# Attention diagonal by four products instead of a DRAM round trip, and other moves in the first 45 microseconds of a four-layer graph kernel

## Chip, cores and metric

One Trainium2 chip, one of its cores. The metric is the device time of one execution in microseconds (us), median of several runs of the same program; lower is better. The engines of the core work side by side and wait for each other by semaphores: PE is TensorE (matrix products; PEld loads its weights), DVE is VectorE, ACT is ScalarE, POOL is GpSimd, and SP is the queue that asks for transfers (DMA). Products land in PSUM, eight banks of 128x512 float32.

## The reference, cut to what matters

`x` has 32 batches of 512 nodes with 128 features, `adj` is 512x512. Four layers follow each other, each of the form x = x + layer(relu(layernorm(x))). Only the first layer, and its preparation, is touched by the change:

```python
# --- layer 0, as computed on h = relu(layernorm(x)) ---
h0 = jnp.einsum('bnf,fg->bng', h, W[0])
h1 = jnp.einsum('bnf,fg->bng', h, W[1])
m = adj > 0
idx = jnp.cumsum(m.reshape(-1).astype(jnp.int32)) - 1      # running number of the non-zeros
A = softmax(jnp.where(m, e[0][idx], NEG), axis=1)          # the attention matrix, 512 x 512
M = jnp.eye(512)
out = einsum('ij,bjg->big', A * M, h0) + einsum('ij,bjg->big', A * (1 - M), h1) + bias
# layer 1: Chebyshev hops with adj; layer 2: messages with adj*adj; layer 3: masked attention
```

So layer 0 needs the attention matrix without its diagonal (it multiplies h1), and its diagonal by itself: row i of h0 is scaled by A[i, i].

## The kernel before: the parts that the change touches

Batches are handled in pairs, q = 0 to 15, and two pairs make a round r. The kernel is written in the order in which each engine works its instructions off in this part, so the order of lines below is the order on each engine. Blocks of 128 nodes are numbered t.

The inputs are asked for on one queue, and the statistics of the first two pairs are made by DVE and POOL together:

```python
for t in range(NT):
    nc.sync.dma_start(adj_s[:, t, :], adj_r[:, t, :])
# then, on the same queue: x of the first batches, q, k, e, the weights, the other x
...
def early_stats(q, whole):
    for b in range(2):
        for k in range(2 * b, 2 * b + 2):
            nc.vector.bn_stats(st[:, k], xt[q][:, b, ...])
        if whole and b == 0: yield; continue
        nc.vector.tensor_scalar(sd[:, half], st[:, half, :, 2], 1.0 / D, EPS, OP.mult, OP.add)
        nc.vector.tensor_scalar(sh[:, half], st[:, half, :, 1], -1.0, None, OP.mult)
        nc.gpsimd.tensor_tensor(rs[:, half], sd[:, half], minus_half[:, half], OP.pow)
        nc.gpsimd.tensor_mul(sh[:, half], sh[:, half], rs[:, half])
        yield
```

`normal[q]` are the eight ACT instructions that make h of pair q from x, shift and scale. `pe_steps` (`turned[q]`) turns h of a pair: eight PE transposes into two banks at the first step, then a copy of each bank into hT. `project_steps` (`project[q]`) multiplies hT with W[1] into two banks, and copies both into g. Then comes the numbering of the non-zeros, with the turning of pair 0 behind it:

```python
pw = [bank(f"p_upto_{kk}") for kk in range(NK)]            # running sums, NK = 2
for kk in range(NK):
    for j in range(NT): nc.tensor.matmul(pw[kk][:, j * P :], pgs[:, j, blk(kk)], upto[:, j, j * P :], ...)
turned = [pe_steps(h[q], f"hT0_{q}", hT[q], copies[q]) for q in range(3)]
next(turned[0])                                            # eight transposes of pair 0
next(early[1])
for kk in range(NK):                                       # column of each of the first 256 non-zeros
    nc.vector.tensor_scalar(s, pw[kk], rest[:, kk : kk + 1], None, OP.is_le, OP.add, accum_out=col_of[...])
for kk in range(NK):                                       # one-hots of row and column
    nc.vector.tensor_scalar(at_row[:, kk, :], cols, row_of[:, kk : kk + 1], None, OP.is_equal)
    nc.vector.tensor_scalar(at_col[:, kk, :], cols, col_of[:, kk : kk + 1], -1.0, OP.is_equal, OP.mult)
for kk in range(NK):
    for i in range(3): nc.vector.tensor_scalar(at_part[:, i, kk, :], ...)
go(turned[0])                                              # both ACT copies of pair 0
next(project[0])                                           # products of pair 0 with W[1]
go(normal[1])
```

For each block of rows t the scores are made on PE from the one-hots (`score_rows`), the softmax by DVE and ACT (`softmax_rows`, `inverse`, `scaled_rows`), and the diagonal is cut out and summed:

```python
def scaled_rows(t):
    nc.scalar.mul(split(att[:, t, :]), crossed(us[t]), total[:, t : t + 1])

def without_diagonal(t):
    own = split(att[:, t, :])[:, :, t, :]                  # the block that holds the diagonal
    d = diag[:, t, :]
    nc.vector.tensor_tensor_reduce(d, own, ident, 1.0, 0.0, OP.mult, OP.add, diag_of[:, t : t + 1])
    nc.gpsimd.tensor_sub(own, own, d)
...
without_diagonal(3)
...
# diag_of has one number per node, nodes along the partitions; adiag has all 512 along the free
# dimension, the same on every partition. The way from one to the other leads through DRAM:
nc.sync.dma_start(diag_d.rearrange("(t p) -> p t", p=P), diag_of)
nc.sync.dma_start(adiag[0], AP(diag_d, ap=[[0, P], [1, N]]))
```

Round 0 multiplies the attention matrix with g in seven block products (a Strassen scheme, `ORDER0`: k = 1, 2, 6, 5, 7, 4, 3). Other work is placed behind each of them:

```python
if i == 0:   # behind k = 1
    transpose_rows(pt, att, 2); transpose_rows(pt, att, 3); copies of attT, block sums on DVE
elif i == 1: # behind k = 2
    go(normal[2], NT + 1); diagonal_of(0, 0); go(ln3, NT + 1); go(normal[2]); ...
elif i == 2: # behind k = 6
    diagonal_of(0, 1); add(1, 0, 0)
elif i == 3: # behind k = 5
    turn pair 2 (PE, ACT copies); add(0, 1, 1); bias(0); normalise(3); ...
elif i == 4: # behind k = 7
    upper(held["a"]); turn pair 3; add(1, 1, 2); go(projection(2)); normalise(4); bias(1); ...
elif i == 5: # behind k = 4
    go(projection(3)); go(right_of(1)); diagonal_of(1, 0); normalise(5)
```

`diagonal_of(r, b)` makes hd = hT * adiag on POOL for both pairs of the round (128x512 each). `upper` multiplies hd with W[0] on PE and adds the result to x on DVE; `add` and `bias` are POOL additions of 128x512 into x; `right_of(1)` are the four POOL differences of g that round 1 needs. After round 0 the kernel goes on through seven more rounds of layer 0 and through layers 1 to 3.

Of the kernel before, what the change touches and what calls it, by code (L numbers as in the profile page):

```python
# [16 lines left out]
P = 128  # L17
# [7 lines left out]
def kernel(  # L25
# [51 lines left out]
    def bank(name):  # L77
        return psum.tile([P, 512], F32, tag="bank", name=name)
# [4 lines left out]
    def blk(t):  # L83
        return slice(t * P, (t + 1) * P)
# [17 lines left out]
    adj_s = square_tile("adj_s")  # L102
    adj_r = adj.rearrange("(t p) j -> p t j", p=P)
    for t in range(NT):
        nc.sync.dma_start(adj_s[:, t, :], adj_r[:, t, :])

    xq, xt = [], []

# [70 lines left out]
    nc.scalar.activation(prep.tile([P, 1], F32, name="powers"), eps, AF.Exp)  # L179
    minus_half = const.tile([P, NT, 2], F32, name="minus_half")  # L180
    nc.vector.memset(minus_half, -0.5)

    known = prep.tile([P, NT, 2], F16, name="known")
    nc.vector.tensor_copy(known[:, :, 1], rows)
# [11 lines left out]
    def early_stats(q, whole):  # L196

        st = stats.tile([P, NT, 2, 3], F32, tag="bn", name=f"bn_{q}", bufs=4)
        sd = stats.tile([P, NT, 2], F32, tag="sd", name=f"sd_{q}", bufs=4)
        rs = stats.tile([P, NT, 2], F32, tag="rs", name=f"rs_{q}")  # L200
        sh = stats.tile([P, NT, 2], F32, tag="sh", name=f"sh_{q}")
        shift[q] = sh.rearrange("p k e -> p (k e)")
        scale[q] = rs.rearrange("p k e -> p (k e)")
        for b in range(2):
            for k in range(2 * b, 2 * b + 2):
                t = 2 * k % NT
                nc.vector.bn_stats(st[:, k].rearrange("p e s -> p (e s)"),
                                   xt[q][:, b, t : t + 2, :].rearrange("p t f -> p f t"))
            if whole and b == 0:
                yield  # L210
                continue
            half = slice(0 if whole else 2 * b, 2 * b + 2)
            nc.vector.tensor_scalar(sd[:, half], st[:, half, :, 2], 1.0 / D, EPS, OP.mult, OP.add)
            nc.vector.tensor_scalar(sh[:, half], st[:, half, :, 1], -1.0, None, OP.mult)
            nc.gpsimd.tensor_tensor(rs[:, half], sd[:, half], minus_half[:, half], OP.pow)
            nc.gpsimd.tensor_mul(sh[:, half], sh[:, half], rs[:, half])
            yield
# [41 lines left out]
    def pe_steps(h, name, hT, copy=nc.scalar.copy):  # L259
        ps = [bank(f"p_{name}_{b}") for b in range(2)]  # L260
        for b in range(2):
            for t in range(NT):
                nc.tensor.transpose(ps[b][:, blk(t)], h[:, b, t, :], ident)
        yield
        for b, p in enumerate(ps):
            (copy[b] if isinstance(copy, tuple) else copy)(
                hT[:, :, b, :].rearrange("p b (a c) -> p b a c", c=QR), crossed(p))
            yield
# [178 lines left out]
    def project_steps(q, hT, copy=nc.scalar.copy):  # L447
        r, w = divmod(q, 2)
        if w == 0:
            if r % 3 == 2:  # L450
                g[r] = square_tile(f"g_{r}").rearrange("p t (b w f) -> p t b w f", b=2, w=2)
            else:
                t = quad_tile(f"g_{r}").rearrange("p w e -> p (w e)")[:, : 4 * N]
                g[r] = t.rearrange("p (t b w f) -> p t b w f", t=NT, b=2, w=2)
        pg = [projected(f"p_g_{q}_{b}", (at(hT, b), w0[:, 1, :])) for b in range(2)]
        yield
        for b in range(2):
            copy(g[r][:, :, b, w, :], pg[b])
            yield
# [122 lines left out]

    rest = prep.tile([P, NK], F32, name="rest")
    nc.vector.tensor_sub(rest, rows[:, :NK], pb[:, :, 0])
    pw = [bank(f"p_upto_{kk}") for kk in range(NK)]
    for kk in range(NK):
        for j in range(NT):
# [1 line left out]
                             start=(j == 0), stop=(j == NT - 1), skip_group_check=True)  # L589
    copies = [nc.scalar.copy, (nc.scalar.copy, nc.vector.tensor_copy), nc.scalar.copy]  # L590
    turned = [pe_steps(h[q], f"hT0_{q}", hT[q], copies[q]) for q in range(3)]
    project = [project_steps(q, hT[q], c) for q, c in ((0, nc.scalar.copy), (1, nc.vector.tensor_copy))]
    next(turned[0])
    col_of = prep.tile([P, NK], F32, name="col_of")
    at_row = prep.tile([P, NK, N], BF16, name="at_row")
    at_col = prep.tile([P, NK, N], BF16, name="at_col")
    at_part = prep.tile([P, 3, NK, N], BF16, name="at_part")
    us = [prep.tile([P, N], F32, tag="u", name=f"u_{t}", bufs=NT) for t in range(NT)]
    next(early[1])
    for kk in range(NK):  # L600
        s = prep.tile([P, N], F16, tag="scr", name=f"scr_c{kk}", bufs=2)
        nc.vector.tensor_scalar(s, pw[kk], rest[:, kk : kk + 1], None, OP.is_le, OP.add,
                                accum_out=col_of[:, kk : kk + 1])
    for kk in range(NK):
        nc.vector.tensor_scalar(at_row[:, kk, :], cols, row_of[:, kk : kk + 1], None, OP.is_equal)
        nc.vector.tensor_scalar(at_col[:, kk, :], cols, col_of[:, kk : kk + 1], -1.0, OP.is_equal, OP.mult)
    for kk in range(NK):
        for i in range(3):
            nc.vector.tensor_scalar(at_part[:, i, kk, :], cols, col_of[:, kk : kk + 1],
                                    parts[i][:, kk : kk + 1], OP.is_equal, OP.mult)  # L610
    go(turned[0])
    next(project[0])
    go(normal[1])


    diag = prep.tile([P, NT, P], F32, name="diag")
    diag_of = prep.tile([P, NT], F32, name="diag_of")
    least = prep.tile([P, NT], F32, name="least")
    total = prep.tile([P, NT], F32, name="total")

# [21 lines left out]

    def scaled_rows(t):
        nc.scalar.mul(split(att[:, t, :]), crossed(us[t]), total[:, t : t + 1])

    def without_diagonal(t):

        own = split(att[:, t, :])[:, :, t, :]
        d = diag[:, t, :].rearrange("p (b c) -> p b c", c=QR)
        nc.vector.tensor_tensor_reduce(d, own, ident.rearrange("p (b c) -> p b c", c=QR), 1.0, 0.0,  # L650
                                       OP.mult, OP.add, diag_of[:, t : t + 1])
        nc.gpsimd.tensor_sub(own, own, d)

    attT = square_tile("attT")
# [12 lines left out]
    softmax_rows(2)  # L667
    inverse(1)
    scaled_rows(1)
    without_diagonal(0)  # L670
    score_rows(3)
    next(turned[1])
    next(turned[1])
    softmax_rows(3)
    without_diagonal(1)
    inverse(2)
    scaled_rows(2)
    go(early_stats_2, 2)
    inverse(3)
    scaled_rows(3)  # L680
    next(project[1])
    without_diagonal(2)
    pt = [bank(f"p_attT_{j}") for j in range(NT)]
    transpose_rows(pt, att, 0)
    transpose_rows(pt, att, 1)
    next(project[1])
    without_diagonal(3)
    next(project[1])

    adiag = [work.tile([P, N], F32, tag="rt", name="adiag", bufs=6)]  # L690
    diag_d = bounce.tile([N], F32, tag="diag", name="diag_d", bufs=1)
    tc.keep_in_program_order(nc.sync.dma_start(diag_d.rearrange("(t p) -> p t", p=P), diag_of))
    tc.keep_in_program_order(nc.sync.dma_start(
        adiag[0], bass.AP(tensor=diag_d.tensor, offset=diag_d.offset, ap=[[0, P], [1, N]])))
    left_of_att = att_sums()
    next(left_of_att)
    att_copies((0, 0, nc.scalar.copy), (1, 0, nc.vector.tensor_copy),
# [37 lines left out]

    ahead = {q: stats_steps(q) for q in range(4, NQ)}
    ln3 = stats_steps(3)
    own, turning, hd = {}, {}, {}
    sums_ahead = late_sums()

    def normalise(q):
# [34 lines left out]
    def round0(r):  # L776

        now = rights.pop(r)  # L780
        A, C = 2 * r, 2 * r + 1

        def x_of(I, b):
# [41 lines left out]
        for i, _ in enumerate(products(f"l0_{r}", by_token, sums["att"], now, evict,  # L825
                                          ORDER if r else ORDER0)):
            if r == 0:
                if i == 0:
                    transpose_rows(pt, att, 2)
                    transpose_rows(pt, att, 3)  # L830
                    att_copies((0, 1, nc.scalar.copy), (1, 1, nc.vector.tensor_copy))
                    next(left_of_att)
                    next(left_of_att)
                    go(early_stats_2)
                    att_copies((2, 1, nc.scalar.copy), (3, 1, nc.scalar.copy))
                elif i == 1:
                    go(normal[2], NT + 1)
                    diagonal_of(0, 0)
                    go(ln3, NT + 1)
                    go(normal[2])  # L840
                    next(left_of_att)
                    next(left_of_att)
                    next(squares)
                    go(ln3)
                elif i == 2:
                    diagonal_of(0, 1)
                    add(1, 0, 0)
                elif i == 3:
                    next(turned[2])
                    go(turned[2])  # L850
                    add(0, 1, 1)
                    bias(0)
                    normalise(3)
                    go(ahead[4], NT)
                    go(squares)
                elif i == 4:
                    upper(held["a"])
                    turned.append(pe_steps(h[3], "hT0_3", hT[3]))
                    next(turned[3])
                    go(ahead[4])  # L860
                    add(1, 1, 2)
                    go(turned[3])
                    go(projection(2))
                    normalise(4)
                    go(ahead[5], NT)
                    bias(1)
                    go(turn(4))
                    go(ahead[5])
                elif i == 5:
                    go(projection(3))  # L870
                    go(right_of(1))
                    diagonal_of(1, 0)
                    normalise(5)
                elif i == 6:
                    go(stats_c, NT)
                continue
# [326 lines left out]
```

## Time and profile before

| | before |
|---|---|
| time, median of 3 runs (lowest to highest) | 971.69 us (971.6 to 972.12) |
| span of the profiled execution | 969.8 us |
| PE busy | 956.3 us, 99% |
| PEld busy | 782.4 us, 81% |
| DVE busy | 586.8 us, 61% |
| ACT busy | 469.3 us, 48% |
| POOL busy | 419.4 us, 43% |
| mean granted clock of PE | 0.996 |

A row of the stage table gives, for a stretch of the span, how long each engine was busy in it (in brackets the number of instructions), the clock that PE was granted as a share of full speed, the busy share of the transfer engines, and what they moved. A row of the waits gives an instruction, what it waited for, the total in us, how often, and the longest. A row of an engine's timeline gives start, duration, engine, line, operation, what it writes and reads, how many instructions are merged in it, and in square brackets how long the engine stood idle before it and for whom. "L773" is line 773 of the kernel before. Busy time of an engine that runs beside PE costs nothing by itself; it matters where PE waits for it.

### The profile page before, as it was taken

Reading aid. Unit: us, or ns where it says so; the run is one execution under the profiler, and the core shown is the slowest. Engines: PE = TensorE matmul, PEld = TensorE weight load, DVE = VectorE, ACT = ScalarE, POOL = GpSimd, SP = SyncE. Lnnn points to the kernel's source line nnn. Section 1 sums busy time; section 2 is a strip of 40 time slices with the busy share of each in tenths; the row PEclk is TensorE's granted clock in tenths of the full one; section 3 lists DMA queues with packets and bytes.
Section 4 is the critical chain, followed back from the end, with each engine's and each line's share of the span. In section 5 each row is a group of like instructions: output and inputs, shape, how many; then the busy total and the mean of one; then the engine's idle time right before and its main releaser. Section 6 shows DMA issues by size and latency. Waiting matters only on the chain.

```text
span 969.8 us, 15152 instructions
## 1 busy us (share of the span) xinstructions
PE 956.3 (99%) x5461; PEld 782.4 (81%) x5461; DVE 586.8 (61%) x1339; ACT 469.3 (48%) x1054; POOL 419.4 (43%) x459
## 2 busy tenths in 40 slices
PE   8899999999999999999999999999999999999998
PEld 4699999989999998899887777777676777777776
DVE  8778886746555546646757666656654454454444
ACT  5674442442341242376636744455664445544553
POOL 4486998834328523511424444334042233223322
PEclk9899999999999999999999999999999999999999
DMA  9345643252232321433342432232231121221111
GB/s 250 71 119 164 183 122 110 58 139 66 80 120 62 88 49 39 131 92 102 75 119 81 142 88 70 83 88 75 56 98 55 53 73 51 60 71 44 55 33 44
DMA packets 84586, 86.32 MB, mean 89 GB/s; under 512 B 7328, under 2 KB 75168, under 8 KB 84512
## 3 DMA queue, kind: packets, MB, share of 16 engines
q1 hardware_dynamic: 84512, 85.36, 31.4%
q8 instruction: 43, 0.70, 0.3%
q14 instruction: 31, 0.25, 0.1%
HBM read 44.44 MB, written 40.90 MB: 88 GB/s over the span
## 4 chain that ended last, share of the span: by engine, by line
PE 93%; DVE 3%; DMA 2%; ACT 1%; issue 0%; SPq 0%; POOL 0%; DVEq 0%; ACTq 0%
PE p_av L1123 12%; PE p_score L1108 11%; PE p_l_c L384 8%; PE p_w L433 6%; PE p_l_d L384 5%; PE p_msgT_c L377 4%; PE p_x1T_c L377 4%; PE p_l_a L384 4%; PE p_l L433 3%; PE p_feat L433 3%; PE p_hv L433 3%; PE p_qkh L1095 3%; PE p_x1T_a L377 3%; PE p_msgT_d L377 3%; PE p_x1T_d L377 3%; PE p_msgT_a L377 3%
## 5 line engine op out<-in xcount | busy, mean ns | idle before, releaser
L245 ACT ACTIVATE h<-x,sh,rs 128x128 f32<-128x128 f32 x512 | 209.1, 485 | 54.8 <-DVE sh L234 23.9
L1113 POOL TENSOR_TENSOR ex<-ex,adjTx 128x512 f32<-128x512 f32 x62 | 80.3, 1296 | 208.2 <-ACT ex L1111 208.2
L1109 ACT ACTIVATE ex<-p_score 128x512 f32<-128x512 f32 x128 | 71.8, 587 | 122.9 <-issue 113.1
L1123 PEld LDWEIGHTS p_av<-qkh_hv,ex 128*128 128x128 f32 x1024 | 118.4, 191 | 8.4 <-issue 7.4
L1123 PE MATMUL p_av<-qkh_hv,ex 128*128 128x129 f32 x1024 | 119.9, 274 | 0.0
L1108 PE MATMUL p_score<-qkh_hv,hT 128*128 128x512 f32 x256 | 115.2, 593 | 0.0
L281 DVE STREAM_TRANSPOSE hb_hT<-h 128x512 f32<-128x512 f32 x120 | 82.0, 698 | 23.6 <-ACT h L245 23.2
L1113 DVE TENSOR_TENSOR ex<-ex,adjTx 128x512 f32<-128x512 f32 x66 | 46.1, 702 | 82.0 <-ACT ex L1111 81.9
L225 DVE BATCH_NORM_STATS2 bn<-x 128x6 f32<-128x256 f32 x248 | 89.7, 416 | 0.6
L1108 PEld LDWEIGHTS p_score<-qkh_hv,hT 128*128 128x128 f32 x256 | 46.2, 190 | 46.5 <-issue 44.5
L1111 ACT ACTIVATE ex<-ex 128x512 f32<-128x512 f32 x128 | 76.6, 630 | 1.8
L354 POOL TENSOR_TENSOR rt_feat<-feat,feat 128x256 f32<-128x256 f32 x16 | 11.6, 726 | 136.3 <-ACT feat L1062 136.3
L956 ACT COPY w<-p_w 128x512 f32<-128x512 f32 x32 | 18.2, 574 | 105.6 <-PE p_w L433 105.6
L354 POOL TENSOR_TENSOR rt_w<-w,rt_w 128x512 f32<-128x512 f32 x16 | 20.4, 1276 | 110.2 <-DVE rt_w L354 91.8
L433 PE MATMUL p_w<-th,x1T 128*128 128x128 f32 x256 | 49.5, 275 | 0.0
L433 PE MATMUL p_w<-th,hs 128*128 128x128 f32 x256 | 49.5, 275 | 0.0
L433 PEld LDWEIGHTS p_hv<-vw,hT 128*128 128x128 f32 x256 | 33.6, 192 | 15.3 <-issue 8.1
L1073 POOL TENSOR_TENSOR x<-x,phi2b 128x256 f32<-128x256 f32 x64 | 44.5, 727 | 0.0
L717 POOL TENSOR_TENSOR hd<-hT,adiag 128x512 f32<-128x512 f32 x32 | 39.7, 1276 | 8.2 <-DMA adiag<-diag_d 8.2
L433 PEld LDWEIGHTS p_w<-th,hs 128*128 128x128 f32 x256 | 39.9, 192 | 0.7
L1128 DVE SCALAR_TENSOR_TENSOR x<-p_av,rsum,x 128x128 f32<-128x128 f32 x128 | 39.1, 346 | 1.9
L1062 ACT ACTIVATE feat<-feat 128x512 f32<-128x512 f32 x32 | 20.1, 629 | 41.4 <-DVE feat L1061 41.4
(231 smaller groups left out, 2041.4 us busy)
## 6 DMA issues: line engine op xcount, KB each, us to landing
d_hT<-hb_hT SPq DMA_DIRECT2D x240, 128.0 KB
hT<-d_hT SPq DMA_DIRECT2D x60, 512.0 KB
x<-in_x_dram SPq DMA_DIRECT2D x32, 256.0 KB
out_dram<-x SPq DMA_DIRECT2D x31, 256.0 KB
adj_s<-in_adj_dram SPq DMA_DIRECT2D x4, 256.0 KB
adjT_d<-adj_squares SPq DMA_DIRECT2D x4, 256.0 KB
sq<-in_adj_dram SPq DMA_DIRECT2D x4, 256.0 KB
adjTx<-adjT_d SPq DMA_DIRECT2D x4, 256.0 KB
```

Of the source, the lines that this page charges most:

```text
L225: nc.vector.bn_stats(st[:, k].rearrange("p e s -> p (e s)"), xt[q][:, b, t : t + 2, :].rearrange("p t f -> p f t"))
L245: nc.scalar.activation(h[:, b, t, :], xt[q][:, b, t, :], AF.Relu, bias=shift[q][:, i : i + 1], scale=scale[q][:, i : i + 1])
L281: nc.vector.transpose(hb[:, :, b].rearrange("p j t r -> p t j r"), h[:, b].rearrange("p t (j c) -> p t j c", c=QR))
L377: nc.tensor.matmul(p[:, :H], b[:, k, :], a[:, k, :], start=(first and k == 0), stop=(k == 1), skip_group_check=True)
L384: nc.tensor.matmul(p[:, i * 2 * D : (i + 1) * 2 * D], a[:, k, blk(i)], b[:, k], start=(first and i == 0 and k == 0), stop=(k == 1), skip_g ...
L433: nc.tensor.matmul(p[:, blk(t)], hT(t), w, start=(i == 0), stop=(i == len(terms) - 1))
L1073: tc.keep_in_program_order(nc.gpsimd.tensor_add(xi, xi, spread(phi2b, 2)))
L1108: nc.tensor.matmul(ps, hT[:, t, b, :], qkh, start=True, stop=True)
L1109: nc.scalar.activation(ex[:, t, :], ps, AF.Tanh, scale=1.0 / (8.0 * math.sqrt(D)))
L1111: nc.scalar.activation(ex[:, t, :], ex[:, t, :], AF.Exp, scale=8.0)
L1113: eng.tensor_mul(split(ex[:, t, :]), split(ex[:, t, :]), crossed(adjTx[0][:, t, :]))
L1123: nc.tensor.matmul(po[:, i, : D + 1], ex[:, t, blk(i0 + i)], hv[:, t, :], start=(t == 0), stop=(t == NT - 1))
```

## The change

Four things are altered. **First**, blocks 1 and 3 of `adj` are asked for on ACT's queue and blocks 0 and 2 on SP's, so that the loads of `x` behind them are asked for sooner. **Second**, the two small steps between the statistics and the power (`sd`, `sh`) and one of the four one-hots of row and column (`at_row[1]`) go from DVE to POOL. **Third**, pair 0 is turned batch by batch: batch 0 before the running sums (its copy behind ACT's copy of `pgs`), batch 1 behind them. **Fourth**, the diagonal block is cut out by a plain POOL multiplication, straight after the row is scaled, and the row of all diagonals on every partition is made by PE: a matrix of ones times the diagonal block leaves the sum of each column, which is the diagonal itself, on every partition. Four such products go into a bank behind k = 2 of round 0, and one ACT copy brings the bank to `adiag`. The sums `diag_of` and the two transfers through DRAM are gone.

```diff
--- before.py
+++ after.py
@@ -102,7 +102,7 @@
     adj_s = square_tile("adj_s")
     adj_r = adj.rearrange("(t p) j -> p t j", p=P)
     for t in range(NT):
-        nc.sync.dma_start(adj_s[:, t, :], adj_r[:, t, :])
+        (nc.scalar if t % 2 else nc.sync).dma_start(adj_s[:, t, :], adj_r[:, t, :])
 
     xq, xt = [], []
 
@@ -179,6 +179,8 @@
     nc.scalar.activation(prep.tile([P, 1], F32, name="powers"), eps, AF.Exp)
     minus_half = const.tile([P, NT, 2], F32, name="minus_half")
     nc.vector.memset(minus_half, -0.5)
+    ones = const.tile([P, P], F32, name="ones")
+    nc.vector.memset(ones, 1.0)
 
     known = prep.tile([P, NT, 2], F16, name="known")
     nc.vector.tensor_copy(known[:, :, 1], rows)
@@ -210,8 +212,8 @@
                 yield
                 continue
             half = slice(0 if whole else 2 * b, 2 * b + 2)
-            nc.vector.tensor_scalar(sd[:, half], st[:, half, :, 2], 1.0 / D, EPS, OP.mult, OP.add)
-            nc.vector.tensor_scalar(sh[:, half], st[:, half, :, 1], -1.0, None, OP.mult)
+            nc.gpsimd.tensor_scalar(sd[:, half], st[:, half, :, 2], 1.0 / D, EPS, OP.mult, OP.add)
+            nc.gpsimd.tensor_scalar(sh[:, half], st[:, half, :, 1], -1.0, None, OP.mult)
             nc.gpsimd.tensor_tensor(rs[:, half], sd[:, half], minus_half[:, half], OP.pow)
             nc.gpsimd.tensor_mul(sh[:, half], sh[:, half], rs[:, half])
             yield
@@ -582,6 +584,13 @@
 
     rest = prep.tile([P, NK], F32, name="rest")
     nc.vector.tensor_sub(rest, rows[:, :NK], pb[:, :, 0])
+    def turn_first(b):
+        p = bank(f"p_hT0_0_{b}")
+        for t in range(NT):
+            nc.tensor.transpose(p[:, blk(t)], h[0][:, b, t, :], ident)
+        nc.scalar.copy(hT[0][:, :, b, :].rearrange("p b (a c) -> p b a c", c=QR), crossed(p))
+
+    turn_first(0)
     pw = [bank(f"p_upto_{kk}") for kk in range(NK)]
     for kk in range(NK):
         for j in range(NT):
@@ -589,32 +598,32 @@
                              start=(j == 0), stop=(j == NT - 1), skip_group_check=True)
     copies = [nc.scalar.copy, (nc.scalar.copy, nc.vector.tensor_copy), nc.scalar.copy]
     turned = [pe_steps(h[q], f"hT0_{q}", hT[q], copies[q]) for q in range(3)]
+    turn_first(1)
     project = [project_steps(q, hT[q], c) for q, c in ((0, nc.scalar.copy), (1, nc.vector.tensor_copy))]
-    next(turned[0])
     col_of = prep.tile([P, NK], F32, name="col_of")
     at_row = prep.tile([P, NK, N], BF16, name="at_row")
     at_col = prep.tile([P, NK, N], BF16, name="at_col")
     at_part = prep.tile([P, 3, NK, N], BF16, name="at_part")
     us = [prep.tile([P, N], F32, tag="u", name=f"u_{t}", bufs=NT) for t in range(NT)]
+    nc.gpsimd.tensor_scalar(at_row[:, 1, :], cols, row_of[:, 1:2], None, OP.is_equal)
     next(early[1])
     for kk in range(NK):
         s = prep.tile([P, N], F16, tag="scr", name=f"scr_c{kk}", bufs=2)
         nc.vector.tensor_scalar(s, pw[kk], rest[:, kk : kk + 1], None, OP.is_le, OP.add,
                                 accum_out=col_of[:, kk : kk + 1])
     for kk in range(NK):
-        nc.vector.tensor_scalar(at_row[:, kk, :], cols, row_of[:, kk : kk + 1], None, OP.is_equal)
+        if kk == 0:
+            nc.vector.tensor_scalar(at_row[:, kk, :], cols, row_of[:, kk : kk + 1], None, OP.is_equal)
         nc.vector.tensor_scalar(at_col[:, kk, :], cols, col_of[:, kk : kk + 1], -1.0, OP.is_equal, OP.mult)
     for kk in range(NK):
         for i in range(3):
             nc.vector.tensor_scalar(at_part[:, i, kk, :], cols, col_of[:, kk : kk + 1],
                                     parts[i][:, kk : kk + 1], OP.is_equal, OP.mult)
-    go(turned[0])
     next(project[0])
     go(normal[1])
 
 
     diag = prep.tile([P, NT, P], F32, name="diag")
-    diag_of = prep.tile([P, NT], F32, name="diag_of")
     least = prep.tile([P, NT], F32, name="least")
     total = prep.tile([P, NT], F32, name="total")
 
@@ -642,13 +651,9 @@
 
     def scaled_rows(t):
         nc.scalar.mul(split(att[:, t, :]), crossed(us[t]), total[:, t : t + 1])
-
-    def without_diagonal(t):
-
         own = split(att[:, t, :])[:, :, t, :]
         d = diag[:, t, :].rearrange("p (b c) -> p b c", c=QR)
-        nc.vector.tensor_tensor_reduce(d, own, ident.rearrange("p (b c) -> p b c", c=QR), 1.0, 0.0,
-                                       OP.mult, OP.add, diag_of[:, t : t + 1])
+        nc.gpsimd.tensor_mul(d, own, ident.rearrange("p (b c) -> p b c", c=QR))
         nc.gpsimd.tensor_sub(own, own, d)
 
     attT = square_tile("attT")
@@ -667,31 +672,20 @@
     softmax_rows(2)
     inverse(1)
     scaled_rows(1)
-    without_diagonal(0)
     score_rows(3)
     next(turned[1])
     next(turned[1])
     softmax_rows(3)
-    without_diagonal(1)
     inverse(2)
     scaled_rows(2)
     go(early_stats_2, 2)
     inverse(3)
     scaled_rows(3)
     next(project[1])
-    without_diagonal(2)
     pt = [bank(f"p_attT_{j}") for j in range(NT)]
     transpose_rows(pt, att, 0)
     transpose_rows(pt, att, 1)
-    next(project[1])
-    without_diagonal(3)
-    next(project[1])
-
-    adiag = [work.tile([P, N], F32, tag="rt", name="adiag", bufs=6)]
-    diag_d = bounce.tile([N], F32, tag="diag", name="diag_d", bufs=1)
-    tc.keep_in_program_order(nc.sync.dma_start(diag_d.rearrange("(t p) -> p t", p=P), diag_of))
-    tc.keep_in_program_order(nc.sync.dma_start(
-        adiag[0], bass.AP(tensor=diag_d.tensor, offset=diag_d.offset, ap=[[0, P], [1, N]])))
+    go(project[1])
     left_of_att = att_sums()
     next(left_of_att)
     att_copies((0, 0, nc.scalar.copy), (1, 0, nc.vector.tensor_copy),
@@ -735,7 +729,7 @@
 
     ahead = {q: stats_steps(q) for q in range(4, NQ)}
     ln3 = stats_steps(3)
-    own, turning, hd = {}, {}, {}
+    own, turning, hd, adiag = {}, {}, {}, []
     sums_ahead = late_sums()
 
     def normalise(q):
@@ -778,6 +772,10 @@
 
 
         now = rights.pop(r)
+        if r == 0:
+
+            adiag.append(work.tile([P, N], F32, tag="rt", name="adiag", bufs=6))
+            p_adiag = bank("p_adiag")
         A, C = 2 * r, 2 * r + 1
 
         def x_of(I, b):
@@ -834,6 +832,9 @@
                     go(early_stats_2)
                     att_copies((2, 1, nc.scalar.copy), (3, 1, nc.scalar.copy))
                 elif i == 1:
+                    for t in range(NT):
+                        nc.tensor.matmul(p_adiag[:, blk(t)], ones, diag[:, t, :], start=True, stop=True)
+                    nc.scalar.copy(adiag[0], p_adiag)
                     go(normal[2], NT + 1)
                     diagonal_of(0, 0)
                     go(ln3, NT + 1)
```

## The prediction

> **What bounds the kernel now.** I read the page first: its 40 slices and the chain that ended last.
>
> ```profile
> PE 956.3 (99%) x5461; PEld 782.4 (81%) x5461; DVE 586.8 (61%) x1339; ACT 469.3 (48%) x1054; POOL 419.4 (43%) x459
> PE   8899999999999999999999999999999999999998
> PEclk9899999999999999999999999999999999999999
> PE 93%; DVE 3%; DMA 2%; ACT 1%; issue 0%; SPq 0%; POOL 0%; DVEq 0%; ACTq 0%
> ```
>
> PE is the bound of the whole span, so only two things bring time: less work on PE, or shorter waits of PE. One slice is 24 us. Only the first two show PE below 9 tenths ahead of the last one, and the second is also the only one with a lower clock after the start. All that the change touches lies in these two. Next I read PE's waits over the whole span, longest first:
>
> ```profile
> PE p_l_a L773 <- POOL hd L717: 3.6, 2, 3.2
> PE p_idle L498 <- DVE upto L187: 2.0, 1, 2.0
> ...
> PE p_g L433 <- DMA hT<-d_hT: 0.5, 1, 0.5
> PE p_upto L588 <- ACT pgs L578: 0.5, 1, 0.5
> PE p_l_c L384 <- DVE u_l L797: 0.4, 1, 0.4
> ```
>
> The longest wait is for hd, which POOL makes from adiag, the diagonal on its way through DRAM. What happens on SP's queue, on POOL and on PE around it, from their timelines:
>
> ```profile
> 29.47 0.38 SPq L692 DMA_DIRECT2D diag_d<-diag_of  x1
> 39.96 0.32 SPq L693 DMA_DIRECT2D adiag<-diag_d  x1
> 43.38 4.92 POOL L717 TENSOR_TENSOR hd<-hT,adiag 128x512 f32<-128x512 f32 x4 [8.17 <-DMA adiag<-diag_d]
> ```
>
> The 2 KB of the diagonal are asked for at 29.47 and only at 39.96 can the second transfer start; adiag is there at 43.38, and POOL has stood idle 8.17 us. PE pays twice:
>
> ```profile
> 39.54 1.96 PE L384 MATMUL p_l_c<-rt_g,attT 128*128 128x256 f32 x8 [0.45 <-DVE u_l L797]
> 44.69 0.80 PE L773 MATMUL p_l_a<-w,hd 128*128 128x128 f32 x2 [3.18 <-POOL hd L717]
> 45.91 1.65 PE L773 MATMUL p_l_a<-w,hd 128*128 128x128 f32 x6 [0.42 <-POOL hd L717]
> 47.35 1.92 PE L263 MATMUL p_hT<-ident,h 128*128 128x128 f32 x8
> 49.06 2.60 PE L433 MATMUL p_g<-w,hT 128*128 128x128 f32 x16
> ...
> 54.12 1.95 PE L433 MATMUL p_g<-w,hT 128*128 128x128 f32 x16
> ```
>
> First 3.18 + 0.42 = 3.6 us idle. Then the same transposes that took 1.04 at 38.06 take 1.92, and p_g 2.60 against 1.95 later. The stage table says why (its columns: stretch, length, PE, PEld, DVE, ACT, POOL busy, clock, transfers):
>
> ```profile
> 41.50:44.60 3.10, 0.01 (x1) 0.00 (x0) 1.70 (x3) 1.54 (x5) 1.22 (x2) 0.84 0.75 161
> 44.60:50.50 5.90, 5.39 (x24) 5.09 (x25) 0.00 (x0) 1.17 (x2) 5.90 (x6) 0.51 0.57 126
> 50.50:60.00 9.50, 9.50 (x70) 9.04 (x69) 6.08 (x15) 7.90 (x20) 6.18 (x6) 1.00 0.18 44
> 80.00:200.00 120.00, 119.78 (x734) 110.02 (x733) 95.40 (x208) 53.55 (x136) 101.23 (x91) 1.00 0.46 126
> ```
>
> The clock is 0.51 for 5.9 us after the wait. From 80 us on PE is busy 119.78 of 120 us: what is won before carries through to the end nearly whole, as no slack swallows it.
>
> **What the Trainium skill says.** "TensorE: Matmul & The Clock Gate", Part 1, says that an idle stretch of about a 3.4 us window halves PE's clock, and that about as much busy time is needed to get it back. The trace agrees: 3.18 us idle, then 0.51 for 5.9 us. "DMA: Bandwidth & Descriptors", section Specifications, puts transfers of less than 512 B among the slow ones; diag_d writes single 4-byte numbers, and its 2 KB took about 10.5 us here, which agrees in kind. The same page, section "Issuing engines are not separate DMA queues", says that asking on two engines saves only the time of asking, since all run on the same 16 engines; the trace agrees in part: between 4 and 8 us those engines are 1.00 busy at 289 GB/s, so they are the limit and not the asking. "GPSIMD Engine Reference", section 4.1, has POOL about twice as slow as DVE for two inputs: the product ex takes 1296 ns on POOL against 702 on DVE.
>
> **Part 1, adj on two queues.** An issue takes SP about 0.45 us, so x is asked for about 0.9 us sooner (1.7 instead of 2.58). But by 7.2 us, when the first x lands, some 1.6 MB have been moved, which is just adj (1.05 MB), two x (0.52) and a little more. The order of data hardly changes. I count 0; ACT's two issues are free, as ACT waits from 2.2 to 8.9 us.
>
> **Part 2, small steps on POOL.** DVE loses sd and sh three times, some 0.2 us each. After the first two DVE reaches lt at 9.2 instead of 9.61. But POOL gets two instructions of some 0.25 us (as its other tiny ones, 0.2 to 0.3) ahead of each power of 1.04, so sh of batch 1 is ready at about 11.8 instead of 11.2. ACT takes 0.4 us per h: batch 0 from 10.18 to 11.8, then batch 1 until 13.4, and pgs behind it at 13.4 to 13.95 against 13.84 before. So the running sums do not start sooner: +0.1. Later, DVE without the third sd/sh (0.16) and without at_row[1] (0.26) ends the one-hots at 18.8 instead of 19.25. at_row[1] on POOL (0.65, from the 617 ns of the POOL scalar step on att) is done by 15.1, needed at 17.
>
> **Part 3, turning by batch.** PE's four transposes of batch 0 (0.44) move into the 0.5 us wait for pgs; its ACT copy (0.59) is done during the sums. So p_g starts at sums 15.2 + transposes 0.46 = 15.7 instead of 16.26: -0.55. The score rows start at 17.75; the sixth part is needed at 19.2 and ready at 18.8, so the gain holds. ACT's h of pair 1 starts 0.5 us later (17.5) and pushes ACT's softmax, so pair 1's hT copy ends at 25.95 instead of 26.15 and PE waits some 0.4 us there; the softmax itself stays at -0.55.
>
> **Part 4a, cutting on POOL.** Two of DVE's `diag` instructions with their waits lie in the chain between 28.3 and 29.4 us. Without them, g's copies run from 27.2 to 28.55, attT's at 28.8 to 29.15. k = 1 then runs without a break from about 29.0 to 30.75, instead of ending at 32.0: **-1.25 in all so far**. POOL needs 0.45 + 0.45 per block, the last done at 29.45, ahead of its need at 30.75. right_of(0) on POOL ends at 34.6, as before within 0.6.
>
> **Part 4b, ones times diagonal.** Four float32 products 128x128, like the L773 groups of four (recorded as x8) with 0.89 us: **+0.9** on PE, ending at 34.25. One ACT copy of 128x512, some 0.57, gives adiag at 34.9 instead of 43.38. ACT makes the rest of h(2) from then, until 38.4; PE's transposes of pair 2 end at 38.6; k = 7 starts 38.65, without the 0.45 wait for DVE (its L797 is now done at 38.0): **-0.45**, and some -0.1 from rounding. k = 7 ends at 40.4 against 41.3.
>
> Now hd: POOL 34.9 to 39.8, so `upper` need not wait: **-3.6**. PE does not cool down: from 44.69 to 51.66 it needed 6.97 us for L773, transposes and p_g, less the 0.42 counted already is 6.55, where 0.89 + 0.87 + 1.79 = 3.55 is the full-speed time by the chain: **-3.0**. But h(3) on ACT now comes at the limit: 39.5 + 3.19 = 42.7, when PE, done with `upper` at 41.3, has one batch turned by 41.75 and waits until then: **+0.9, a new wait** less 0.3 for transposes that run beside it, so +0.6. POOL's additions and bias end at 43.6 (before 51.98), so DVE, ACT's h(4) (45.1 instead of 53.27) and right_of(1) move by 7 to 8 us, as much as PE; they stay just ahead of it.
>
> **Sum.** -1.25 + 0.9 - 0.55 - 3.6 - 3.0 + 0.6 = -6.9, less a little for the ends: 971.7 - 6.7 = **965.0 us**.
>
> **Rivals.** (A) *The wait is replaced.* Once POOL is free at 35, ACT's h(2), h(3), h(4) or DVE's chain can become what PE waits for. For: ACT is busy nearly without a break from 35.27 to 43, DVE 14.47 of 15.5 us from 26 to 41.5. If PE waits 2 to 3 us more, 967 to 968.5. If the wait is long enough to halve the clock again, about 970. (B) *The transfers set the pace.* hT of pair 5 came last at 74.27 after two transfers; if these don't move with the engines, PE waits there for what it won, and the time is 968 to 970. Against: the chain before them is DVE and ACT work that moves by as much. (C) *The start gives more.* If x lands 0.7 us sooner after all, ACT's h and pgs follow and the time is 964. (D) *POOL is slower* on the tiny steps or the comparison (1 us instead of 0.65): the preparation loses 0.5 to 1 us, 966.
>
> **Range and chances.** The two large terms, 3.6 and 3.0, are measured in the trace and have one cause, so most of the weight lies between 963.5 and 967; A and B give the longer tail upward. Range **962.5 to 968.5**. Two per cent are 19.4 us, three times all that is in reach: faster 0.01, same 0.98, slower 0.01.
>
> **What would show it.** Right: no wait of PE for hd, clock 1.00 between 40 and 55 us, k = 1 of round 0 ending near 30.8, a small wait of PE for ACT's h around 42, round 1's first product near 52.6 instead of 59.42. Wrong: half clock anywhere after 10 us, PE waiting for ACT by more than 1 us in this stretch, a wait for hT of pair 5 above 2 us, the running sums starting later than 14.3.

## The result and the profile after

The change takes 964.68 us (median of 6 runs, 964.1 to 964.87), the kernel before 972.26 us in the runs beside it (971.6 to 973.05): a ratio of 0.9921, with a 95% interval of 0.9908 to 0.9934. The spans of the two profiled executions are 969.8 and 962.8 us, 7.0 apart.

First the waits of PE over the whole span, longest first:

```profile
PE p_idle L500 <- DVE upto L189: 2.0, 1, 2.0
PE p_g L435 <- ACT hT L268: 1.3, 1, 1.3
PE p_l_a L386 <- ACT w L957: 0.7, 1, 0.7
...
PE p_upto L597 <- ACT pgs L580: 0.2, 1, 0.2
```

The 3.6 us for hd are gone, and so are the 0.4 for VectorE's u_l ahead of k = 7 and the 0.5 for hT of pair 5. A new wait stands second: 1.3 us for ACT's copy of pair 1, before round 0. POOL's timeline where it stood idle for 8.17 us:

```profile
36.55 4.97 POOL L711 TENSOR_TENSOR hd<-hT,adiag 128x512 f32<-128x512 f32 x4 [1.07 <-ACT adiag L837]
```

It starts 6.83 us sooner than at 43.38. PE from the new products on:

```profile
34.79 1.05 PE L836 MATMUL p_adiag<-diag,ones 128*128 128x128 f32 x8
...
40.01 1.89 PE L386 MATMUL p_l_c<-rt_g,attT 128*128 128x256 f32 x8
41.74 1.05 PE L767 MATMUL p_l_a<-w,hd 128*128 128x128 f32 x8
42.63 1.67 PE L265 MATMUL p_hT<-ident,h 128*128 128x128 f32 x8
44.14 1.95 PE L435 MATMUL p_g<-w,hT 128*128 128x128 f32 x16
45.93 1.89 PE L386 MATMUL p_l_c<-rt_g,attT 128*128 128x256 f32 x8
```

Nothing stands in square brackets any more. p_g takes 1.95 instead of 2.60, at full clock. The transposes of pair 3 take 1.67, which is neither 1.04 nor the 1.92 of the half clock: some of them wait for ACT's h, which ends at 43.92, inside the merged row: 0.63 us more than 1.04, where the prediction foresaw a new wait of 0.6. The stage table:

```profile
38.00:41.00 3.00, 3.00 (x20) 2.69 (x19) 2.97 (x10) 2.97 (x9) 3.00 (x3) 1.00 0.02 5
41.00:44.00 3.00, 2.89 (x21) 2.30 (x20) 2.49 (x5) 3.00 (x9) 3.00 (x4) 1.00 0.26 52
44.00:53.00 9.00, 9.00 (x66) 8.59 (x67) 4.80 (x12) 8.46 (x22) 5.41 (x5) 1.00 0.63 132
```

The clock column reads 1.00 in each stretch. Where the 7.0 us come from is read by following the same instructions through both traces:

| instant on PE | before | after | shift |
|---|---|---|---|
| start of the running sums | 13.88 | 14.43 | +0.55 |
| end of k = 1 of round 0 (start plus length of its last row) | 31.99 | 32.17 | +0.18 |
| start of k = 7 | 39.54 | 40.01 | +0.47 |
| start of k = 4 (behind `upper`, turning of pair 3, p_g) | 51.50 | 45.93 | -5.57 |
| first product of round 1 | 59.42 | 53.85 | -5.57 |
| first product of round 2 | 79.67 | 73.16 | -6.51 |
| end of the span | 969.8 | 962.8 | -7.0 |

So all the preparation, three of the four parts of the change among it, gives nothing in this pair of traces. Between k = 7 and k = 4 6.04 us are won. Another 0.94 follow in round 1, of which 0.54 is the recorded wait for hT that stood at 74.27, and 0.5 are spread over the rest of the span.

### The profile page after: what moved, and what is told of

Same layout as the page of the kernel before. It is cut to its first block, busy times and chain, and to the rows that moved or that the text cites. A ratio compares the mean times of both kernels' runs of the same rounds, so it can differ in the third digit from the quotient of the medians.

```text
span 962.8 us, 15161 instructions
## 1 busy us (share of the span) xinstructions
PE 954.6 (99%) x5469; PEld 781.1 (81%) x5469; DVE 584.5 (61%) x1325; ACT 469.5 (49%) x1055; POOL 424.7 (44%) x470
## 4 chain that ended last, share of the span: by engine, by line
PE 96%; ACT 2%; POOL 1%; DVE 1%; issue 0%; DVEq 0%; POOLq 0%; ACTq 0%
PE p_av L1124 12%; PE p_score L1109 11%; PE p_l_c L386 8%; PE p_w L435 6%; PE p_l_d L386 6%; PE p_msgT_c L379 5%; PE p_l_a L386 4%; PE p_x1T_c L379 4%; PE p_l L435 3%; PE p_feat L435 3%; PE p_hv L435 3%; PE p_msgT_d L379 3%; PE p_msgT_a L379 3%; PE p_phi L1079 3%; PE p_qkh L1096 3%; PE p_phi L1080 3%
```

## The experiments

Two theories were to be told apart. **M**: all the gain hangs on the way of the diagonal through DRAM, and the other parts are worth nothing together. **P**: the terms of the prediction hold as they were summed, so the turning by batch and the cutting on POOL bring about 1.25 us together, and the half clock costs 3.0 by itself. Times are medians, with the lowest and highest in brackets; kernels of one group ran on one chip beside the kernel before. Where only the ratio is told, its 95% interval stands with it.

### One part alone, all but one part

The fourth part alone (POOL cuts, four products, one ACT copy):

```diff
-    nc.vector.tensor_tensor_reduce(d, own, ident, 1.0, 0.0, OP.mult, OP.add, diag_of[...])
+    nc.gpsimd.tensor_mul(d, own, ident)                      # straight behind scaled_rows
-    two DMAs: diag_of -> diag_d -> adiag[0]
+    for t in range(NT): nc.tensor.matmul(p_adiag[:, blk(t)], ones, diag[:, t, :], start=True, stop=True)
+    nc.scalar.copy(adiag[0], p_adiag)                        # behind k = 2 of round 0
```

> The kernel before with the fourth part alone: the diagonal cut out on GpSimd and brought to all partitions by four products. Theory M (the gain is the wait for the transfers through DRAM and the half clock behind it, and the three other parts are worth nothing together): as fast as the whole change or a little faster, 964 to 965 us, 6.7 to 8 us under the kernel before. Rival P (my prediction as it was summed: the three other parts bring about 0.5 us of their own before the softmax, and the rest of the 1.25 comes with the cutting on GpSimd): 0.5 us slower than the whole change, 965.2 to 966.

Measured: 964.34 us (964.21 to 965.11), ratio 0.9923 (0.9909 to 0.9937), against the 0.9921 of the whole change. This is what M expects. The intervals reach 1.3 to 1.4 us to either side, so these times alone don't exclude the 0.5 us that P expects of the other parts; against P stands the trace of the change, +0.18 us at the end of k = 1 where P has -1.25. The second run is the whole change with just this part taken out again:

> The whole change without its fourth part: adj on two queues, small steps and one one-hot on GpSimd, pair 0 turned batch by batch, but the diagonal summed by VectorE and sent through DRAM as before. Theory M: within 0.6 us of the kernel before, or slower, since the product of pair 1 waits for ScalarE, whose h came late from GpSimd. Rival P: 0.5 us or more faster than before, as the sums and transfers start that much sooner.

Measured: 971.37 us, ratio 1.0000 (0.9992 to 1.0009). Three parts of the change together are worth less than 0.1% (0.9 us) either way. Their trace has the 1.3 us wait too, and then the old one:

```profile
PE p_l_a L783 <- POOL hd L727: 3.0, 2, 2.3
PE p_idle L500 <- DVE upto L189: 2.0, 1, 2.0
PE p_g L435 <- ACT hT L268: 1.3, 1, 1.3
```

The third run keeps the four products but has DVE do the cutting, as before:

```diff
     # fourth part alone, but
-    nc.gpsimd.tensor_mul(d, own, ident)
+    nc.vector.tensor_tensor_reduce(d, own, ident, 1.0, 0.0, OP.mult, OP.add, diag_of[...])   # four, between other DVE work
```

> As the run of the fourth part alone, but the diagonal is still cut out and summed by VectorE (the sums are read by nobody now): only the way through DRAM is replaced by four products. Tells what the cutting on GpSimd is worth by itself. By my prediction VectorE's cutting lies in the chain ahead of the first product of round 0 and costs about 0.7 us: 0.7 slower than with the cutting on GpSimd. Rival (round 0 is then bound by VectorE's block sums and by ScalarE, which hide it): no difference, within 0.3 us.

Measured: 965.30 us (964.85 to 966.09), 0.96 above the fourth part alone, where 0.7 was expected; the two ranges overlap a little. PE's k = 1 breaks in two again, as in the kernel before:

```profile
29.98 0.70 PE L386 MATMUL p_l_a<-g,attT 128*128 128x256 f32 x2
31.02 1.56 PE L386 MATMUL p_l_a<-g,attT 128*128 128x256 f32 x6 [0.34 <-DVE attT L316]
```

From the start of the running sums to the end of k = 1 this trace needs 18.13 us, that of the fourth part alone 17.53: 0.60 of the difference is seen there. So the cutting on POOL is worth 0.6 to 1 us, and the way through DRAM the other 6. M named the right part of the change, but not all of its gain is the wait for the transfers.

### Which of the three other parts eats the rest

> The whole change once more, unaltered, beside the three runs that undo one thing in it, so that they are compared on one chip: 7 us under the kernel before, 964 to 965.

Measured: 964.78 us (963.83 to 965.05), the reference for the next three, each of which undoes one thing in the whole change.

```diff
-    (nc.scalar if t % 2 else nc.sync).dma_start(adj_s[:, t, :], adj_r[:, t, :])
+    nc.sync.dma_start(adj_s[:, t, :], adj_r[:, t, :])
```

> The whole change, but all four blocks of adj asked for on SP's queue as before. My prediction: no difference. What the trace of the change suggests instead: the first block came at 4.50 us with two queues and at 3.42 with one, so the counting of non-zeros starts 1.1 us sooner with one queue; the running sums gain at most what TensorE's warm-up ahead of them leaves, 0 to 0.5 us, and the product of pair 1 waits for ScalarE anyway: within 0.5 us of the whole change, rather faster.

Measured: 964.86 us (964.52 to 966.21), no difference. The first block does come sooner with one queue, DVE's first counting step starting at 3.48 us against 4.36 with two, but in these two traces the last block comes later (DVE ends at 7.6 against 6.9). The running sums start 0.47 us later with one queue (14.87 against 14.40), and at the first product of round 2 only 0.06 is left of that (73.24 against 73.18).

```diff
-    nc.gpsimd.tensor_scalar(at_row[:, 1, :], cols, row_of[:, 1:2], None, OP.is_equal)
-        if kk == 0:
-            nc.vector.tensor_scalar(at_row[:, kk, :], ...)
+        nc.vector.tensor_scalar(at_row[:, kk, :], ...)
```

> The whole change, but the one-hot of row that went to GpSimd is made by VectorE again. In the change it took 1.58 us on GpSimd and stood ahead of the power of pair 1's statistics, and TensorE waited 1.30 us for ScalarE's copy of pair 1 behind it. Theory Q (this one-hot delays h of pair 1 and so takes back what the turning by batch brought): pair 1's h starts at about 17.6 instead of 19.1, the wait of 1.3 falls below 0.3, and the time falls by 0.7 to 1.2 us under the whole change. Rival (ScalarE's softmax is bound by VectorE's least values, which come 0.26 later with the one-hot on VectorE): within 0.3 us.

Measured: 963.63 us (963.45 to 963.82), 1.15 below the whole change, and its highest run is just below the lowest of that. Within this group theory Q holds. In the change POOL's timeline ahead of pair 1's h reads:

```profile
14.71 1.58 POOL L608 TENSOR_SCALAR at_row<-cols,row_of 128x512 bf16<-128x512 f16 x1
16.37 0.20 POOL L215 TENSOR_SCALAR sd<-bn 128x8 f32<-128x8 f32 x1
16.65 0.33 POOL L216 TENSOR_SCALAR sh<-bn 128x8 f32<-128x8 f32 x1
16.95 1.79 POOL L217 TENSOR_TENSOR rs<-sd,minus_half 128x8 f32<-128x8 f32 x1
18.82 0.26 POOL L218 TENSOR_TENSOR sh<-sh,rs 128x8 f32<-128x8 f32 x1
```

and ACT's h of pair 1 behind it, first in the change, then with the one-hot back on DVE:

```profile
19.11 3.19 ACT L247 ACTIVATE h<-x,sh,rs 128x128 f32<-128x128 f32 x8 [2.36 <-POOL sh L218]
```

```profile
17.81 3.19 ACT L247 ACTIVATE h<-x,sh,rs 128x128 f32<-128x128 f32 x8 [1.02 <-POOL sh L218]
```

The h starts 1.30 us sooner (0.99 sooner than in the repeat of the change, where it started at 18.80), and the wait of PE for the copy of pair 1, 1.30 us in the change and 0.97 in its repeat, is absent from that run's waits. The size of the gain is less sure than its cause: by the ratio to the kernel before, this run (0.9920, 0.9906 to 0.9933) and the change in its two groups (0.9921 and 0.9930) can't be told apart.

```diff
-    turn_first(0)          # ahead of the running sums
-    turn_first(1)          # behind them
+    next(turned[0])        # all eight transposes behind them, both copies behind the one-hots
```

> The whole change, but pair 0 turned in one go behind the running sums, as before. My prediction: 0.55 us slower than the whole change. By theory Q the turning's gain ends in the 1.3 us wait of pair 1's product for ScalarE: within 0.2 us of the whole change, with that wait 0.4 to 0.6 shorter.

Measured: 965.10 us (964.07 to 965.7) against 964.78, no difference that these runs show. The wait for the copy of pair 1 is 0.19 in its trace against 0.97 in the other: what the turning won, ACT was not ready to use.

### Is the half clock a cost by itself?

Products that nobody reads fill the wait of the kernel before; nothing else is altered, and adiag arrives no sooner.

```diff
+    p_fill = bank("p_fill")
+    for _ in range(6):     # three in the second run
+        nc.tensor.matmul(p_fill, ident, adj_s[:, 0, :], start=True, stop=True)
     upper(held["a"])
```

> The kernel before with six more float32 products of 128x512 on TensorE, whose bank nobody reads, placed right ahead of the products that wait for hd; by the 0.45 us per such product of the score lines they fill some 2.7 us of the 3.2 us wait. They add nothing to the result and shorten no wait. If the slow stretch behind the wait comes from TensorE being idle: the granted clock stays at 1.00 through 40 to 55 us, the transposes of pair 3 take about 1.0 us instead of 1.92, and the time falls by about 3 us, to 968.5 to 969.5, with the other 3.6 us still lost to the wait. Rival (the slow stretch comes from the transfers or from GpSimd working beside TensorE): the same half clock and 972, or later by what the products take.

Measured: 971.36 us, ratio 0.9995 (0.9987 to 1.0004). The clock is 1.00 in each stretch of the table from 38 to 60 us, and the transposes of pair 3 take 1.04: the slow stretch does come from PE being idle. But no time is won. I had sized the filling wrongly: a score row counts two records, so a product takes 0.86 us and the six ended 2 us behind hd. Hence the same with three:

> The kernel before with three float32 products of 128x512 that nobody reads in TensorE's wait for hd, instead of six: at the 0.86 us each that the six took, 2.6 us inside the wait of 3.2. Theory S (the half clock is worth little by itself: behind adiag GpSimd's hd, additions and bias, then VectorE, ScalarE's h of pair 4 and GpSimd's differences form a chain of their own, which sets rounds 0 and 1 as much as TensorE does): clock 1.00, the first product of round 1 at about 56.5 instead of 59.4, but then waits for GpSimd's differences and for hT that take 2 to 3 us back; time 970.5 to 971.5. My prediction's term (the half clock costs 3.0 us by itself): 968 to 968.7.

Measured: 972.01 us, ratio 0.9999 (0.9990 to 1.0007). Again full clock and no gain. The stretch that was at 0.51 in the kernel before:

```profile
44.60:50.50 5.90, 4.86 (x37) 4.57 (x38) 0.00 (x0) 2.25 (x4) 5.90 (x6) 1.00 0.65 137
```

PE shows where the time goes:

```profile
41.66 2.74 PE L859 MATMUL p_fill<-adj_s,ident 128*128 128x512 f32 x6
44.91 0.49 PE L773 MATMUL p_l_a<-w,hd 128*128 128x128 f32 x2 [0.51 <-POOL hd L717]
46.13 0.94 PE L773 MATMUL p_l_a<-w,hd 128*128 128x128 f32 x6 [0.73 <-POOL hd L717]
46.90 1.04 PE L263 MATMUL p_hT<-ident,h 128*128 128x128 f32 x8
...
57.57 1.89 PE L384 MATMUL p_l_a<-g,attT 128*128 128x256 f32 x8
60.61 1.99 PE L384 MATMUL p_l_c<-rt_g,sums_att 128*128 128x256 f32 x8 [1.15 <-POOL rt_g L354]
...
64.91 2.02 PE L433 MATMUL p_g<-w,hT 128*128 128x128 f32 x16 [0.58 <-DMA hT<-d_hT]
...
74.71 2.05 PE L433 MATMUL p_g<-w,hT 128*128 128x128 f32 x16 [0.81 <-DMA hT<-d_hT]
```

Round 1 starts at 57.57 instead of 59.42, and then PE waits 1.15, 0.58 and 0.81 us for things that POOL, ACT and the transfers made no sooner. POOL got adiag when it always did, and its four hd, two additions and a bias must end before DVE, ACT's h of pair 4 and POOL's differences for round 1 follow. That chain is about as long as PE's at half clock. The kernel before, without any filling, says the same: of its 74 executions beside these runs 41 had a mean granted clock of 0.996 and 31 one of 0.998 (two had 1.000), and the medians of these groups are 971.44 and 971.69 us. By an estimate from these figures the 0.002 between them are 1.9 us of clock in 970 us, and no time shows for them. The last two runs were to shorten the chain, without and with the three products:

```diff
-    diagonal_of(0, 1)                  # POOL, behind k = 6
+    diagonal_of(0, 1, nc.vector)       # DVE, ahead of upper, where it stood idle
```

> The kernel before, but two of the four hd of round 0 are made by VectorE, ahead of its addition of the first block, where it stood idle for 8.8 us: GpSimd's chain behind adiag is 2.5 us shorter, the way through DRAM and the half clock stay. Theory S: TensorE at half clock is then the longer of the two; only the later wait for hT of 0.5 us can go: 970.5 to 971.2. If GpSimd's chain alone were what counts: 969.

> Both at once: the three products in the wait, and two of the four hd on VectorE. Theory S: now both limits behind adiag are shorter, so the time falls by 2 to 3 us, to 968.3 to 969.5, though each alone brings nearly nothing. My prediction's term: the same as with the three products alone.

Measured: with DVE's help alone 971.62 us (970.13 to 972.52), ratio 0.9996 (0.9988 to 1.0004); with both 970.25 us (969.37 to 972.58), ratio 0.9988 (0.9981 to 0.9995). Neither limit alone brings anything that these runs show, both together 1.2 us by the ratio. That is the direction of theory S, and less than the 2 to 3 us it named. The profiled execution of the second:

```profile
45.72 0.49 PE L773 MATMUL p_l_a<-w,hd 128*128 128x128 f32 x2 [0.93 <-POOL hd L717]
47.38 1.65 PE L773 MATMUL p_l_a<-w,hd 128*128 128x128 f32 x6 [1.18 <-POOL hd L717]
```

The two hd on POOL took 3.45 us instead of 2.5 while DVE made its two in 2.35, so PE waited 1.18 for the second (0.73 with the three products alone), and the clock fell to 0.50 all the same. But this execution, at 971.56 us, is not typical. It is one of four of the 20 with a mean granted clock of 0.998, and the median of these four is 971.46 us; the other 16 had 0.999 or 1.000 and a median of 970.18. So with POOL's chain shortened the loss of clock goes with about 1.3 us, by few executions whose ranges overlap, and still less than the 3.0 of the prediction. That restoring the clock alone brings nothing is shown twice.

### The whole second part undone

```diff
     # whole change, with sd, sh and at_row[1] all back on nc.vector
```

> The whole change, but all that went from VectorE to GpSimd ahead of the softmax goes back: the small steps of the statistics and the one-hot. What stays is adj on two queues, the turning by batch, and the diagonal by four products with its cutting on GpSimd. With the one-hot back the time was 963.6; with the small steps back ScalarE's h of pair 0 and the copy of the running numbers behind it can start up to 0.6 us sooner, where TensorE waited 0.2 to 1.4 us for that copy: 963.0 to 963.6. Rival (TensorE's warm-up ahead of it decides): as with the one-hot alone, 963.6.

Measured: 964.60 us (964.31 to 964.7), ratio 0.9922 (0.9909 to 0.9936), beside a kernel before that was at 971.78 in this group and at 971.19 in the earlier one. By the ratio it equals the run with the one-hot alone (0.9920), but the 963.0 to 963.6 that was expected is missed. Its trace shows a new wait:

```profile
38.27 1.00 DVE L236 SCALAR_TENSOR_TENSOR sh<-bn,rs 128x8 f32<-128x8 f32 x1
40.02 1.96 PE L386 MATMUL p_l_c<-rt_g,attT 128*128 128x256 f32 x8 [0.87 <-DVE u_l L793]
```

The running sums started at 13.49 us, against 14.47 with only the one-hot back on DVE, but k = 1 ended only 0.16 sooner, at 31.14. Then a small DVE step (the shift of a later pair), beside POOL's hd, took 1.00 us against 0.21 in that other trace; DVE's u_l came late, and PE waited 0.87 for it, so that k = 7 started at 40.02 against 39.14. So the time shows nothing for the small steps on either engine. In the traces the running sums start at 14.04 us on average with the small steps on DVE (eight traces, 13.49 to 14.58) and at 14.45 with them on POOL (six, 14.07 to 14.87), some 0.4 later; the kernels differ in other parts too, so the cause of that is not shown.

## Why the prediction was right, step by step

**The total was right, 965.0 against 964.68, but partly because two errors cancel.**

*The diagonal's way* (-3.6, -3.0, +0.6, so -6.0): measured -6.04 between k = 7 and k = 4. The mechanism is shown by the fourth part alone, which has the whole gain, and by the change without it, which has none. What was wrong is the reading of 3.6 and 3.0 as two costs that add. With full clock and the same arrival of adiag the time stays: PE's slow stretch lay beside POOL's chain from the same arrival. The two terms were right to add only because the change moves adiag itself and with it both.

*The four products* (+0.9, then -0.45 for the wait before k = 7, -0.1): from the end of k = 1 to the start of k = 7 it took 7.55 us before and 7.84 after, +0.29 against +0.35 predicted.

*The preparation* (-1.25 by the end of k = 1): **this step failed**; measured +0.18. It is the sum of four shifts between the two traces. The running sums started 0.55 later, where the prediction had +0.1. From there to the end of the score rows, where the turning by batch acts, 0.83 were won (they ended at 25.82 instead of 26.10). PE's wait for the copy of pair 1 took 1.18 back: p_g started at 27.12 instead of 26.22. From there to the end of k = 1, where the cutting acts, 0.72 were won, as predicted (0.7). The term that was mis-sized most is the wait, through the one-hot on POOL, "0.65, from the 617 ns of the POOL scalar step on att": it took 1.58 us, in each trace that has it. It stands ahead of POOL's power of pair 1's statistics, so h of pair 1 started at 19.1 and not at 17.5, and PE waited 1.30 us for its copy where the prediction had "some 0.4". Of the 1.6 us by which h was later than predicted, 0.93 are the size of the one-hot. That the one-hot causes the wait is shown by its return to DVE, and that the turning's gain ended in this wait by the undoing of the turning. Adj on two queues was worth nothing, as predicted.

*What came on top*: 0.94 us in round 1 and 0.5 later, which the sum did not have. The prediction let hT of pair 5 move along with PE; in fact its chain moved further than PE, and the wait of 0.54 vanished. These 1.4 us make up for the 1.4 that the preparation failed to bring, and that is luck.

Of the rivals, A (the wait is replaced) came true before round 0 and not behind it, D (POOL slower) came true for the comparison, and B (transfers) came out the other way round. Of the signs that the prediction named, the wait for hd is gone and the clock is 1.00 from 40 to 55 us. But k = 1 ended at 32.17 and not near 30.8, round 1 began at 53.85 and not near 52.6, and one sign of being wrong came true: the running sums started at 14.43, later than 14.3.

## What to carry to other kernels

A wait of the bounding engine is worth removing at its source: here the arrival that ended it also started a second chain beside it, and shortening one of the two brought nothing. When work moves to an engine that has time, look at what stands behind it in that engine's order, not only at its busy share. Take a duration for it only from the same operation and types; here a neighbour of the same shape was off by a factor of 2.4. And a profile shows one execution: see from the times and clocks of the others whether it is a typical one.

## What was not expected of the hardware

- GpSimd's comparison of 128x512 float16 with a number per partition, into bfloat16, took 1.58 us; its add-and-multiply of 128x512 float16 into float32 took 0.62 us; VectorE makes the comparison in 0.35 us.
- With both transfer queues in use, the first of four 256 KB blocks was ready for DVE at 4.22 to 4.50 us in six traces, against 3.40 to 3.65 with one queue in eight. DVE had counted the last one at 6.9 to 7.1 us with two and at 6.4 to 7.7 with one.
- GpSimd and VectorE multiplying 128x512 float32 side by side: in the profiled execution with the three products POOL took 1.71 and 1.78 us, where its median is 1.27, and DVE 0.68 and 1.76; with DVE's help alone POOL took 1.27 and 1.71 and DVE 1.69 and 1.75, where its product ex took 702 ns.
- The clock fell before a wait of 3.4 us was over, and kept to a grid. In the kernel before it went to 0.50 at 43.6 us, 2.1 us after PE's last product had ended (41.50), and came back at 50.4, 6.8 us later; 0.51 from 44.60 on, as the prediction reads it, is the later part of this. In the change without its fourth part and in the two runs with DVE's help it stayed low for 3.4 us each. In the one of these that has the three products as well, waits of 0.93 and 1.18 us with 0.49 of work between were enough; with the three products alone, 0.51 and 0.73 were not. The Trainium skill, "TensorE: Matmul & The Clock Gate", Part 1, speaks of an idle window of about 3.4 us that is free-running. The lengths of the low stretches, one and two such windows, fit that, and so does their place: from the turn of the warm-up products to the fall 37.5, 37.5, 41.0 and 41.0 us pass in these four traces, 11 and 12 times 3.41. But the window need not be wholly idle: about 2 us of waiting in it were enough here.
- The sixteen products that warm PE up at the start, in which nothing differs between the kernels, took 4.95 to 6.57 us in the 14 traces. The moment at which they turn from about 0.43 to 0.22 us each varies: near 6 us in the profile before and near 8 in the profile after, where DVE then waited 0.82 us for the product behind them. So part of the 0.55 us by which the running sums start later in that profile need not come from the change.
